# Maxima for a softmax: TensorE transposes replaced by VectorE's 32x32 block transposes, with four partial values a query

## The chip, the core and the metric

The kernel runs on one core of one Trainium2 chip. A core has five engines that run beside each other, each with its own in-order stream of instructions: TensorE (PE; its weight loads are listed as PEld), VectorE (DVE), ScalarE (ACT), GpSimd (POOL) and SyncE (SP). In this kernel SP issues all DMAs. An engine waits for another through semaphores, and whatever stands behind a waiting instruction on the same engine waits too. The metric is device time in microseconds (us); lower is better.

## What is computed

Cross-attention, then a state-space mixer, then a routed low-rank layer, each added to `x` (8 sequences of 64 tokens, width 512). The change touches only the softmax of the cross-attention:

```python
    q = rmsnorm(hidden @ q_proj_w.T)            # 32 heads of 128
    k, v = context @ k_proj_w.T, context @ v_proj_w.T   # 8 key heads, 1601 keys
    scores = einsum('bhqd,bhkd->bhqk', q, rmsnorm(k)) / sqrt(128) + mask
    attn = softmax(scores)                      # over the 1601 keys
    out = einsum('bhqk,bhkd->bhqd', attn, v)
```

Softmax takes the maximum over the keys off every score before the exponential. All data is float32.

## The kernel before

**Units.** The attention is cut into 32 units, 4 pairs of key heads (`pr`) for each of 8 sequences (`b`), `pr` running fastest. A pass of the loop in `attend_all` does two things at once: it projects keys and values of unit n (nine "pieces", the P of the list below), and it does the attention of unit n-1. The order in which a pass is written is a list:

```python
    order = (
        "S00 P S01 P S02 P A0 D P S10 B0 P S11 P S12 V00 N A1 P V01 B1 F P P V10 V11".split()
    )
```

The digit after a letter is the half (0 or 1): one of the unit's two key heads, with 4 query heads x 64 queries = 256 query columns. S makes scores, A the maxima, B the softmax, V the product with the values. N and F are sums and factors for the norm of the keys, and D is the division by the softmax's sums.

**The framework's planner.** The list is not yet the order on the engines. Semaphores and buffers come from a tile framework. It takes the place in the program as a priority and puts each engine's instructions in order ahead of time, from its own estimate of when each is ready. On the chip that order is fixed: an engine does not pass over an instruction whose input is late.

**Scores (S, lines 526 to 542).** Keys lie on partitions, queries along the free axis: TensorE makes tiles of 128 keys x 256 queries (13 tiles for 1601 keys; PSUM buffer `psc`, two of them). VectorE multiplies each by the key's norm factor and adds the mask (L531) into `attn`, and keeps a running maximum of two tiles at a time (L540, L542).

**Maxima (A, lines 547 to 564).** L549 and L550 leave `mx`, 128 partitions x 256 queries: what is still to be taken is the maximum over the 128 partitions. TensorE transposes `mx` in two blocks of 128x128 into PSUM (`mtp`, L553), VectorE takes the maximum along the free axis and negates it (L555, `nm`), and a VectorE transpose (L558, 32x32 blocks) turns the column into four rows per block. SP writes the 256 values to a buffer in DRAM (L562, `max_d`) and, once the write has landed, loads them from there into all 128 partitions (L564, `nbs`, 128 KB).

**Softmax (B, lines 570 to 588).** ScalarE copies `nbs` to PSUM (L571, `nb`), VectorE adds it to four tiles at a time (L574, the last at L584), ScalarE takes the exponential (L578, L585), GpSimd sums over the tiles (L580 to L588).

**Buffers.** `mtp`, `nb` and the keys' squared sums `psn` (L414, copied out by ScalarE at L419) share one PSUM buffer, tag `tr` of the pool `ps3`, with a single copy.

**The projections around it.** A piece makes products in four PSUM banks (`pk_a` to `pk_d` for keys, L385; `pv_a` to `pv_d` for values, L445), and between them VectorE takes sums off (L359 `u`, L361 `t`, L377). The second half of a piece adds onto banks that these sums must have read: `pk_b` waits for L361, `pk_c` for L377. At the change from one sequence to the next, a pass also loads the next context (L826, `cx`, two loads of 768 KB, issued after A0 in the list, the other parts later in the pass) and VectorE forms sums of it (L849). These passes are called context passes here, and the others ordinary passes.

Of the kernel before, what the change touches and what calls it, by code (L numbers as in the profile page):

```python
# [9 lines left out]
F32 = mybir.dt.float32  # L10
AF = mybir.ActivationFunctionType
ALU = mybir.AluOpType
AX = mybir.AxisListType
PSUM = bass.MemoryType.PSUM

P = 128
# [37 lines left out]
def key_rows(t):  # L54

    return P if t < 2 * NHT else KV - 2 * NHT * P
# [57 lines left out]
def load_ln_exp(nc):  # L114

    return nc.scalar.preload_act_table_set("natural_log_exp_and_others")
# [186 lines left out]
def attend_all(  # L303
# [7 lines left out]
    nc = tc.nc  # L311

    wk2 = ctx.enter_context(tc.tile_pool(name="xa_wk2", bufs=2))
    small = ctx.enter_context(tc.tile_pool(name="xa_small", bufs=4))
    kp = ctx.enter_context(tc.tile_pool(name="xa_k", bufs=2))
    vp = [ctx.enter_context(tc.tile_pool(name="xa_v0", bufs=1))]
    ap_ = ctx.enter_context(tc.tile_pool(name="xa_attn", bufs=2))
# [3 lines left out]
    ps3 = ctx.enter_context(tc.tile_pool(name="xa_ps3", bufs=1, space=PSUM))  # L321
# [3 lines left out]
        pass  # L325


    negated = [wk2.tile([P, 2, 32], F32, tag=f"nm{hh}", name=f"nm{hh}", bufs=1) for hh in range(2)]
    for nm in negated:
        nc.gpsimd.memset(nm, 0.0)  # L330

# [1 line left out]
    marks = {}  # L333
# [172 lines left out]
    def attention(u):  # L506
# [37 lines left out]
        def maxima(hh):  # L544

            s = st[hh]
            at, lr = s.at, key_rows(NKT - 1)
            mx = ap_.tile([P, 256], F32, tag="mx", name="mx")
            nc.vector.tensor_tensor(mx, s.mx2[:, 0, :], s.mx2[:, 1, :], ALU.max)  # L549
            nc.vector.tensor_tensor(mx[:lr], mx[:lr], at[:lr, NKT - 1, :], ALU.max)  # L550
            tp = ps3.tile([P, 2, P], F32, tag="tr", name="mtp")
            for i in range(2):
                nc.tensor.transpose(tp[:, i, :], mx[:, i * P : (i + 1) * P], c.ident)  # L553
            nm = negated[hh]
            nc.vector.tensor_reduce(nm[:, :, 0], tp, axis=AX.X, op=ALU.max, negate=True)  # L555

            turned = small.tile([P, 2, 32], F32, tag="nmt", name="nmt")
            nc.vector.transpose(  # L558
                turned.rearrange("p i q -> p (i q)"), nm.rearrange("p i q -> p (i q)")
            )  # L560
            row = u.rows.maxima[hh]
            nc.sync.dma_start(out=row.rearrange("(i a q) -> a i q", i=2, q=32), in_=turned[0:P:32])  # L562
            s.nbs = ap_.tile([P, 256], F32, tag="nbs", name="nbs")
            marks["load"] = nc.sync.dma_start(out=s.nbs, in_=row.rearrange("(o q) -> o q", o=1).broadcast_to([P, 256]))  # L564

        def softmax(hh):
            s = st[hh]
            at, lr = s.at, key_rows(NKT - 1)

            nb = ps3.tile([P, 256], F32, tag="tr", name="nb")  # L570
            nc.scalar.copy(nb, s.nbs)  # L571
            sm2 = ap_.tile([P, 2, 256], F32, tag="sm2", name="sm2", bufs=1)
            for k in range(0, NKT - 1, 4):
                nc.vector.tensor_tensor(  # L574
                    at[:, k : k + 4, :], at[:, k : k + 4, :],
                    nb.unsqueeze(1).to_broadcast([P, 4, 256]), ALU.add,
                )
                nc.scalar.activation(at[:, k : k + 4, :], at[:, k : k + 4, :], AF.Exp)  # L578
                if k == 0:
                    nc.gpsimd.tensor_tensor(sm2, at[:, 0:2, :], at[:, 2:4, :], ALU.add)  # L580
                else:
                    for i in (k, k + 2):
                        nc.gpsimd.tensor_tensor(sm2, sm2, at[:, i : i + 2, :], ALU.add)  # L583
            nc.vector.tensor_tensor(at[:lr, NKT - 1, :], at[:lr, NKT - 1, :], nb[:lr], ALU.add)  # L584
            marks["exp"] = nc.scalar.activation(at[:lr, NKT - 1, :], at[:lr, NKT - 1, :], AF.Exp)  # L585
            s.sm = ap_.tile([P, 256], F32, tag="sm", name="sm")
            nc.gpsimd.tensor_tensor(s.sm, sm2[:, 0, :], sm2[:, 1, :], ALU.add)
            nc.gpsimd.tensor_tensor(s.sm[:lr], s.sm[:lr], at[:lr, NKT - 1, :], ALU.add)  # L588
# [43 lines left out]
        def divide():  # L632
# [9 lines left out]
            S00=lambda: score(0, s0), S01=lambda: score(0, s1), S02=lambda: score(0, s2),  # L642
            S10=lambda: score(1, s0), S11=lambda: score(1, s1), S12=lambda: score(1, s2),
            A0=lambda: maxima(0), A1=lambda: maxima(1),
            B0=lambda: softmax(0), B1=lambda: softmax(1),
            V00=lambda: outputs(0, 0), V01=lambda: outputs(0, 1),
            V10=lambda: outputs(1, 0), V11=lambda: (outputs(1, 1), sums()),
# [8 lines left out]
    for n in range(NPR * B):  # L656
        u = Unit()
# [108 lines left out]
    for n in range(len(units) + 1):  # L766
        if n < len(units):
            u = units[n]
            pieces, keys_norms, keys_factors = projections(u)
            todo = ahead(n + 1)  # L770
        else:
            u, pieces = None, last_pieces
# [127 lines left out]
@with_exitstack  # L900
def cross_attention(ctx, tc, c, x, ctxT, lastT, maskT, wq, wk, wv, wo):

    nc = tc.nc
    load_ln_exp(nc)
    big = ctx.enter_context(tc.tile_pool(name="xa_big", bufs=1))
    dram = ctx.enter_context(tc.tile_pool(name="xa_dram", bufs=1, space=bass.MemoryType.DRAM))
    qw = big.tile([P, 1], F32, name="qw")

    nc.vector.tensor_scalar(
        qw, c.qnw, c.knw, 1.0 / math.sqrt(HD), op0=ALU.mult, op1=ALU.mult  # L910
    )
    mask_sb = big.tile([P, NKT, S], F32, name="mask_sb")

    last_keys = big.tile([P, DC, B], F32, name="last_keys")
    q_d = [dram.tile([B, P, PQ, S], F32, name=f"q_d_{pr}") for pr in range(NPR)]
    rs_d = [dram.tile([4, NT], F32, name=f"rs_d_{n}") for n in range(HQ // 4)]
    s_d = {
        (name, pr): dram.tile([P, 4, 2, HD], F32, name=f"{name}_s_d_{pr}")
        for name in ("wk", "wv") for pr in range(NPR)
    }  # L920
    o_d = [dram.tile([P, PQ, B, S], F32, name=f"o_d_{pr}") for pr in range(NPR)]
    v1_d = [dram.tile([B, 2 * HD], F32, name=f"v1_d_{pr}") for pr in range(NPR)]

    rows_d = []
    for i in range(3):
        r = Consts()
        r.keys = dram.tile([4, NHT * P], F32, name=f"keys_d_{i}")
        r.last = dram.tile([4, LAST], F32, name=f"last_d_{i}")
        r.maxima = [dram.tile([256], F32, name=f"max_d_{i}_{hh}") for hh in range(2)]
        r.sums = dram.tile([2, 256], F32, name=f"sums_d_{i}")  # L930
        rows_d.append(r)

    with tc.tile_pool(name="xa_ctx", bufs=1) as ctxp, tc.tile_pool(name="xa_w", bufs=1) as wpool:
        loads = Loads(nc, ctxp, wpool, ctxT, wk, wv, s_d)
        queries_loaded = project_queries(tc, c, x, wq, qw, q_d, rs_d)
        full = NKT - 1

        def load_mask():
            nc.sync.dma_start(
                out=mask_sb[:, :full, :], in_=maskT[: full * P, :].rearrange("(t p) q -> p t q", p=P)  # L940
            )
            nc.sync.dma_start(out=mask_sb[: KV - full * P, full, :], in_=maskT[full * P :, :])
            nc.sync.dma_start(out=last_keys, in_=lastT.rearrange("(dc p) b -> p dc b", p=P))

        return attend_all(
            tc, c, x, loads, mask_sb, load_mask, last_keys, q_d, o_d, v1_d, rows_d, wo, queries_loaded
        )
# [403 lines left out]
@with_exitstack  # L1351
def perceiver(
    ctx: ExitStack, tc, x_in, ctxT, lastT, maskT, wq, wk, wv, wo, small, w_in, w_out, w_ra, b_w, out,
):
    nc = tc.nc
    cpool = ctx.enter_context(tc.tile_pool(name="consts", bufs=1))
    x = cpool.tile([P, NTT, D], F32, name="x")
    for tt in range(NTT):
        nc.sync.dma_start(out=x[:, tt, :], in_=x_in[tt * P : (tt + 1) * P, :])
    c = make_consts(nc, cpool, small)  # L1360
    done = cross_attention(tc, c, x, ctxT, lastT, maskT, wq, wk, wv, wo)
    mixer_and_routed(tc, c, x, done, w_in, w_out, w_ra, b_w, out)
# [52 lines left out]
```

## Time and profile before

| | |
|---|---|
| median of 3 runs | 2828.47 us (2826.2 to 2830.78) |
| the profiled execution | 2826.02 us, of which the traced span is 2824.3 us |
| VectorE busy | 1745.4 us, 62% of the span |
| ScalarE busy | 726.6 us, 26% |
| GpSimd busy | 833.9 us, 30% |
| chain that ended last, by engine | PE 83%, DVE 6%, DMA 2%, ACT 1% |
| same, lines of the attention | `pav` L596 12%, `psc` L526 11%, `nbs<-max_d` 2%, L574 1% |
| running maxima, L542, 128x512 | 818 ns mean, 256 of them |
| L549, 128x256 | 437 ns mean, 64 of them |
| `nb` copy on ScalarE, L571 | 376 ns mean, 64 of them |
| bytes moved by DMA | 206.02 MB, 73 GB/s over the span |

Busy time is the sum of instruction durations on an engine. Matmuls are pipelined: their listed duration is from start to end of one, longer than the distance between two starts in a row. The chain of waits goes back from the last instruction to whatever released it; its shares say where time is on the path that sets the end. A row of the groups gives a source line, the engine, the output and inputs, shapes and count, then total and mean time, then the engine's idle time ahead of it and what ended it. Times in a timeline are us from the start of the span.

### The profile page before, as it was taken

The page shows a single profiled execution, that of the slowest core. Times are in us where ns is not written, and L with a number is a line of the kernel's source. Part 1 is how long each engine was busy: PE and PEld are TensorE (multiplying, and loading weights), DVE is VectorE, ACT ScalarE, POOL GpSimd, SP SyncE. Part 2 cuts the span into 40 slices and gives each one's busy share as a digit, 9 for nine tenths or more (in the row PEclk, how much of TensorE's full clock was granted, in tenths as well). Part 3 has the DMA queues.
Part 4 walks back from the last instruction along what each step waited for, and adds up shares of the span by engine and source line. Part 5 has one row for each costly group of instructions (what it writes and reads, how often), then busy time and mean ns, then how long its engine had stood idle before and what let it go on. Part 6 is the DMA issues. An engine that isn't in the chain of part 4 may idle for free.

```text
span 2824.3 us, 38454 instructions
## 1 busy us (share of the span) xinstructions
PE 2788.6 (99%) x14972; PEld 1980.9 (70%) x14972; DVE 1745.4 (62%) x3059; ACT 726.6 (26%) x1314; POOL 833.9 (30%) x786
## 2 busy tenths in 40 slices
PE   9899999999999999999999999999999999999998
PEld 7677777777777777777777777777777554444444
DVE  4556676676667666665666676667665416444555
ACT  3322223222222222232222222222222103222222
POOL 4323223222222332223222222322232223433431
PEclk9999999999999999999999999999999999999999
DMA  4822232232113122312311131122212441112200
GB/s 164 276 78 57 76 74 53 53 94 53 46 46 97 46 54 79 74 48 58 94 50 50 46 95 47 46 83 76 48 46 72 146 160 38 53 53 78 79 16 15
DMA packets 277230, 206.02 MB, mean 73 GB/s; under 512 B 155676, under 2 KB 240538, under 8 KB 276026
## 3 DMA queue, kind: packets, MB, share of 16 engines
q1 hardware_dynamic: 277050, 203.57, 25.2%
q8 instruction: 119, 1.95, 0.3%
q14 instruction: 61, 0.50, 0.1%
HBM read 180.87 MB, written 22.66 MB: 72 GB/s over the span
## 4 chain that ended last, share of the span: by engine, by line
PE 83%; DVE 6%; DMA 2%; ACT 1%; issue 0%; POOL 0%; SPq 0%; ACTq 0%; DVEq 0%
PE pav L596 12%; PE psc L526 11%; PE pj L1105 8%; PE pv_a L445 6%; PE pv_b L445 6%; PE pv_c L445 5%; PE pk_a L385 5%; PE pk_b L385 5%; PE pk_c L385 5%; PE mo L1213 4%; PE pv_d L445 3%; PE pk_d L385 2%; PE psn L414 2%; DMA nbs<-max_d 2%; DVE attn L574 1%; PE pvl L468 1%
## 5 line engine op out<-in xcount | busy, mean ns | idle before, releaser
L531 DVE SCALAR_TENSOR_TENSOR attn<-psc,rk,mask_sb 128x256 f32<-128x256 f32 (+1 forms) x832 | 363.4, 473 | 190.5 <-PE psc L526 188.1
L580 POOL TENSOR_TENSOR sm<-attn 128x512 f32<-128x512 f32 x64 | 82.0, 1281 | 1147.6 <-ACT attn L578 1147.6
L596 PE MATMUL pav<-attn,v 128*128 128x256 f32 (+1 forms) x1664 | 384.3, 381 | 0.0
L526 PE MATMUL psc<-q,kT 128*128 128x256 f32 x1536 | 371.5, 381 | 0.0
L596 PEld LDWEIGHTS pav<-attn,v 128*128 128x128 f32 (+1 forms) x1664 | 311.1, 190 | 55.4 <-issue 9.6
L583 POOL TENSOR_TENSOR sm<-sm,attn 128x512 f32<-128x512 f32 x256 | 339.8, 1328 | 29.4 <-DVE attn L574 10.6
L526 PEld LDWEIGHTS psc<-q,kT 128*128 128x128 f32 x1536 | 286.3, 190 | 82.4 <-issue 36.0
L1105 PE MATMUL pj<-mx_xnT,w_in 128*128 128x512 f32 x640 | 296.3, 603 | 1.3 <-DVE acc L1122 1.3
L574 DVE TENSOR_TENSOR attn<-attn,nb 128x1024 f32<-128x1024 f32 x192 | 224.7, 1216 | 68.2 <-ACT nb L571 67.9
L445 PEld LDWEIGHTS pv_a<-wv,cx 128*128 128x128 f32 x1536 | 195.5, 191 | 48.2 <-issue 41.4
L578 ACT ACTIVATE attn<-attn 128x1024 f32<-128x1024 f32 x192 | 202.5, 1058 | 71.3 <-DVE attn L574 68.5
L445 PE MATMUL pv_a<-wv,cx 128*128 128x128 f32 x1536 | 212.7, 279 | 0.0
L542 DVE TENSOR_TENSOR mx<-mx,attn 128x512 f32<-128x512 f32 x256 | 209.5, 818 | 2.0
L1105 PEld LDWEIGHTS pj<-mx_xnT,w_in 128*128 128x128 f32 x640 | 115.2, 190 | 129.4 <-issue 124.7
L385 PE MATMUL pk_a<-cx,wk 128*128 128x417 f32 (+1 forms) x512 | 193.3, 500 | 0.8 <-ACT qrs L110 0.8
L396 ACT ACTIVATE ksq<-kT 128x834 f32<-128x834 f32 (+1 forms) x128 | 109.0, 871 | 159.1 <-DVE kT L377 159.1
L637 POOL TENSOR_TENSOR o<-o,f 128x512 f32<-128x512 f32 x31 | 39.4, 1272 | 306.7 <-DMA f<-sums_d 206.3
L385 PEld LDWEIGHTS pk_a<-cx,wk 128*128 128x128 f32 x512 | 97.2, 190 | 46.1 <-issue 20.8
L1217 DVE SCALAR_TENSOR_TENSOR x<-mo,rs,x 128x512 f32<-128x512 f32 x32 | 24.0, 751 | 165.1 <-PE mo L1213 110.4
L1213 PE MATMUL mo<-w_out,y 128*128 128x512 f32 x256 | 118.1, 597 | 0.0
L571 ACT COPY nb<-nbs 128x256 f32<-128x256 f32 x64 | 24.1, 376 | 324.4 <-DMA nbs<-max_d 324.4
L1122 DVE SCALAR_TENSOR_TENSOR acc<-pj,small_consts,acc 128x504 f32<-128x504 f32 (+1 forms) x144 | 103.9, 725 | 0.7
(220 smaller groups left out, 4230.8 us busy)
## 6 DMA issues: line engine op xcount, KB each, us to landing
wk<-in_wk SPq DMA_DIRECT2D x32, 512.0 KB
wv<-in_wv SPq DMA_DIRECT2D x32, 512.0 KB
w_in<-in_w_in SPq DMA_DIRECT2D x16, 1024.0 KB
wvs<-wv_s_d SPq DMA_DIRECT2D x28, 512.0 KB
wks<-wk_s_d SPq DMA_DIRECT2D x28, 512.0 KB
cx<-in_ctxT SPq DMA_DIRECT2D x16, 834.0 KB
cx<-in_ctxT SPq DMA_DIRECT2D x16, 768.0 KB
wq<-in_wq SPq DMA_DIRECT2D x16, 512.0 KB
```

Source lines behind the costliest of these rows:

```text
L385: nc.tensor.matmul(ps[:, :w], lhsT=u.wk[l][:, dc, :], rhs=u.cx.r[ch][r][:, dc, :], start=start and dc == 0, stop=dc == 1, skip_group_check ...
L396: nc.scalar.activation(sq[ch][:, :, half, :w], u.kT[:, :, half, lo:hi], AF.Square)
L445: nc.tensor.matmul(ps[:, i * HD : (i + 1) * HD], lhsT=u.cx.r[ch][r][:, dc, i * P : (i + 1) * P], rhs=u.wv[l][:, dc, :], start=start and i ...
L526: nc.tensor.matmul(ps[:rows, t - t2, :], lhsT=lhsT, rhs=qh, start=True, stop=True)
L531: nc.vector.scalar_tensor_tensor(out=s.at[:rows, t, :].rearrange("p (h q) -> p h q", h=GQ), in0=ps[:rows, t - t2, :].rearrange("p (h q) -> ...
L542: nc.vector.tensor_tensor(s.mx2, s.mx2, s.at[:, t2 : t2 + 2, :], ALU.max)
L574: nc.vector.tensor_tensor(at[:, k : k + 4, :], at[:, k : k + 4, :], nb.unsqueeze(1).to_broadcast([P, 4, 256]), ALU.add,)
L578: nc.scalar.activation(at[:, k : k + 4, :], at[:, k : k + 4, :], AF.Exp)
L583: nc.gpsimd.tensor_tensor(sm2, sm2, at[:, i : i + 2, :], ALU.add)
L596: nc.tensor.matmul(s.av[:, 0, :], lhsT=u.v[:rows, t, hh, :], rhs=s.at[:rows, t, :], start=t == 0, stop=t == NKT - 1,)
L1105: nc.tensor.matmul(pj, lhsT=G.w[:, dc, n, :], rhs=xnT[:, dc, :], start=dc == 0, stop=dc == DC - 1)
L1213: nc.tensor.matmul(po, lhsT=G.y[:, n, tt * P : (tt + 1) * P], rhs=G.wo[:, n, :], start=n == 0, stop=n == GC - 1,)
```

## The change

In A, the TensorE transposes (64 times two) are gone. VectorE transposes `mx` (128x256) in blocks of 32x32 in one instruction into a new SBUF tile `mxt`, and the reduction takes the maximum of each block's 32 columns. Since a block transpose stays within its group of 32 partitions, partition 32i+r, column j then holds the negated maximum of query 32j+r over the keys of partition group i alone: four partial values a query. A second block transpose (128x32 instead of 128x64) lays them out in rows, and SP writes all 128 rows of 32 values (16 KB instead of 1 KB, 128 pieces of 128 bytes instead of 8). The load brings, for each partition, four pieces of 1 KB (512 KB in all instead of 128 KB).

In B, ScalarE's copy is gone. VectorE takes the minimum of the four (they are negated) in two instructions: 128x512 within `nbs`, then 128x256 into the PSUM tile `nb`. `nbs` has one buffer of 4 KB per partition instead of two of 1 KB.

```diff
-    negated = [wk2.tile([P, 2, 32], F32, tag=f"nm{hh}", name=f"nm{hh}", bufs=1) for hh in range(2)]
+    negated = [wk2.tile([P, 32], F32, tag=f"nm{hh}", name=f"nm{hh}", bufs=1) for hh in range(2)]
...
-            tp = ps3.tile([P, 2, P], F32, tag="tr", name="mtp")
-            for i in range(2):
-                nc.tensor.transpose(tp[:, i, :], mx[:, i * P : (i + 1) * P], c.ident)
+
+            tp = ap_.tile([P, 256], F32, tag="mxt", name="mxt", bufs=1)
+            nc.vector.transpose(tp, mx)
             nm = negated[hh]
-            nc.vector.tensor_reduce(nm[:, :, 0], tp, axis=AX.X, op=ALU.max, negate=True)
-
-            turned = small.tile([P, 2, 32], F32, tag="nmt", name="nmt")
-            nc.vector.transpose(
-                turned.rearrange("p i q -> p (i q)"), nm.rearrange("p i q -> p (i q)")
-            )
-            row = u.rows.maxima[hh]
-            nc.sync.dma_start(out=row.rearrange("(i a q) -> a i q", i=2, q=32), in_=turned[0:P:32])
-            s.nbs = ap_.tile([P, 256], F32, tag="nbs", name="nbs")
-            marks["load"] = nc.sync.dma_start(out=s.nbs, in_=row.rearrange("(o q) -> o q", o=1).broadcast_to([P, 256]))
+            nc.vector.tensor_reduce(
+                nm[:, : 256 // 32], tp.rearrange("p (j k) -> p j k", k=32), axis=AX.X, op=ALU.max,
+                negate=True,
+            )
+
+            turned = small.tile([P, 32], F32, tag="nmt", name="nmt")
+            nc.vector.transpose(turned, nm)
+            rows = u.rows.maxima[hh]
+            nc.sync.dma_start(out=rows, in_=turned)
+            s.nbs = ap_.tile([P, 4, 256], F32, tag="nbs", name="nbs", bufs=1)
+            marks["load"] = nc.sync.dma_start(
+                out=s.nbs.rearrange("p i (o q) -> p i o q", o=1),
+                in_=rows.rearrange("(i o j) r -> o i (j r)", i=4, o=1)[:, :, :256]
+                .unsqueeze(2).broadcast_to([P, 4, 1, 256]),
+            )
...
             nb = ps3.tile([P, 256], F32, tag="tr", name="nb")
-            nc.scalar.copy(nb, s.nbs)
+            nc.vector.tensor_tensor(s.nbs[:, 0:2], s.nbs[:, 0:2], s.nbs[:, 2:4], ALU.min)
+            nc.vector.tensor_tensor(nb, s.nbs[:, 0], s.nbs[:, 1], ALU.min)
...
-        r.maxima = [dram.tile([256], F32, name=f"max_d_{i}_{hh}") for hh in range(2)]
+        r.maxima = [dram.tile([P, 32], F32, name=f"max_d_{i}_{hh}") for hh in range(2)]
```

## The prediction

> **What bounds the kernel now.** First the page's busy times, then the rows of the lines that the change touches, out of the groups kept apart by shape:
>
> ```profile
> PE 2788.6 (99%) x14972; PEld 1980.9 (70%) x14972; DVE 1745.4 (62%) x3059; ACT 726.6 (26%) x1314; POOL 833.9 (30%) x786
> ...
> L553 PE MATMUL mtp<-ident,mx 128*128 128x128 f32 x128 | 24.4, 273 | 0.0
> ...
> L555 DVE TENSOR_REDUCE nm<-mtp 128x2 f32<-128x256 f32 x64 | 27.2, 425 | 81.5 <-PE mtp L553 81.5
> ...
> L571 ACT COPY nb<-nbs 128x256 f32<-128x256 f32 x64 | 24.1, 376 | 324.4 <-DMA nbs<-max_d 324.4
> ```
>
> TensorE is the bound over the span, and the transposes are its work. The waits in the other two rows (DVE for the transposes, ACT for the load) count only where TensorE in turn waits for them. Where it does, the chain of waits shows:
>
> ```profile
> 994.92 2.16 PE pav L596 x10
> ...
> 1059.38 2.16 PE pav L596 x10
> ...
> 1107.16 5.52 DMA nbs<-max_d
> 1113.19 3.48 DVE attn L574 x3
> 1122.06 1.95 DVE cs L849
> ...
> 1190.08 2.16 PE pav L596 x10
> ```
>
> From one `pav` mark to the same mark a pass later it is 1059.38 - 994.92 = 64.46 us with nothing but PE between: an ordinary pass, and the trace has 21 that agree to 0.01. The next mark comes at 1190.08, 130.70 us on: 64.47 and a context pass of 66.23, in which the chain leaves PE for the load and then for DVE. Eight context passes lie 1.4 to 3.0 us over 64.47. So the change is worth its PE time in ordinary passes and its load-and-DVE time in context passes.
>
> Third, the timelines, once for an ordinary A0 and B0 and once for a context pass:
>
> ```profile
> 1166.22 0.42 DVE L550 TENSOR_TENSOR mx<-mx,attn 65x256 f32<-65x256 f32 x1
> ...
> 1170.49 0.38 PE L553 MATMUL mtp<-ident,mx 128*128 128x128 f32 x2
> ...
> 1170.71 0.83 PE L445 MATMUL pv_a<-wv,cx 128*128 128x128 f32 x6
> ...
> 1171.64 0.55 SPq L562 DMA_DIRECT2D max_d<-nmt  x1
> ...
> 1173.25 0.32 SPq L564 DMA_DIRECT2D nbs<-max_d  x1
> ...
> 1176.24 0.38 ACT L571 COPY nb<-nbs 128x256 f32<-128x256 f32 x1 [4.18 <-DMA nbs<-max_d]
> ...
> 1176.79 1.21 DVE L574 TENSOR_TENSOR attn<-attn,nb 128x1024 f32<-128x1024 f32 x1
> ...
> 1181.79 0.59 DVE L361 TENSOR_TENSOR t<-u,pk_b 128x417 f32<-128x417 f32 x1
> ...
> 1184.53 1.56 PE L385 MATMUL pk_b<-cx,wks 128*128 128x417 f32 x4
> ```
>
> ```profile
> 1107.16 0.46 SPq L564 DMA_DIRECT2D nbs<-max_d  x1
> ...
> 1113.19 3.48 DVE L574 TENSOR_TENSOR attn<-attn,nb 128x1024 f32<-128x1024 f32 x3 [1.83 <-ACT nb L571]
> ...
> 1125.43 0.62 PE L526 MATMUL psc<-q,kl 128*66 128x256 f32 x2 [1.32 <-DVE attn L531]
> ```
>
> **What goes from TensorE.** The pair of transposes starts at 1170.49, the next matmul at 1170.71: 0.22 us a pair, 64 x 0.22 = 14.1 us. A rule is to be weighed here. The Trainium skill, "TensorE: Matmul & The Clock Gate", Part 4: PE-mode transpose, puts a transpose at about 275 ns in a kernel. The row has 273, but these overlap: by the rule 128 x 0.275 = 35 us would go, by the distance of the starts 14.1. I take 14.1.
>
> **The chain of A.** Now L550 ends at 1166.64 and the write is issued at 1171.64, 5.00 us later (A1 of an ordinary pass: 2.29), because `mtp` waits until ScalarE has emptied `psn` from the shared buffer (that copy runs 1169.86 to 1170.34). The new chain waits for no one: transpose 128x256, reduction, transpose 128x32. The 128x64 transpose takes 245 ns. If a column costs what it costs DVE elsewhere (L542's median 681 ns for 512 columns against L549's 426 for 256: 1.0 ns), 128x256 is 0.44 and 128x32 is 0.21. With 0.43 for the reduction: 1.08, with gaps 1.15. Two evacuations of the value piece (0.55 each) may come between at A0. So the write goes out 1.15 (A1) to 2.2 us (A0) after L550: 1.1 and 2.8 earlier than now.
>
> **The write and the load.** Neither shape is in the trace. Now, write to load is 1.61 us and load to `nb` 2.99 (3.3 at A1). The packet records bound the write: 8 pieces of 128 B are over 1.26 us after issue, a store of 128 pieces of 2 KB 1.66, one of 1024 pieces of 256 B 2.54. So +0 to +1.3; with 128 pieces it is nearest to the second, +0.35. The load of 512 pieces of 1 KB has a twin, `wv`: 3.08 us to its last packet where `nbs` takes 2.87. But `wv` reads different rows at 52 ns a piece and `nbs` the same row at 83 on median; 24 more pieces for each of 16 queues at 83 would be +2.0. So +0.2 to +2.0; I take +0.4, since the `nbs` pieces follow each other at issue speed in both cases. Landing in the ordinary B0: 1166.64 + 2.2 + 1.95 + 3.35 = 1174.15, ahead of the 1176.24 of now.
>
> **The minima on DVE.** 128x512 at 0.68 (L542's median; mean 0.82 with GpSimd beside it), 128x256 at 0.43: 1.1 to 1.25 us for the 0.38 copy on ACT. With +0.40 in A (1.08 for 0.67) DVE gets 1.5 us a half, 64 x 1.5 = 96 us. A rule speaks against exactly this: "VectorE: DVE Perf Modes", Rules for kernel authors, sends 128x128 transposes to TensorE and asks for few DVE operations. Were DVE the bound, the sum would be 96 - 14 = 82 us slower. By this trace DVE is 62% busy and TensorE 99%, so PE time counts in full, and DVE time where DVE runs without a gap.
>
> That is the case at B0. In the ordinary pass DVE is busy from 1175.2 to 1188.4 but for about 0.2 us. Behind the waiting minimum on its in-order stream stand the evacuations of the value piece, the four score tiles of S10, then L574, L359, L361. Until the end of L584 now: 1181.11 (start of L359). After: DVE free at 1173.5, load at 1174.15, about 8 us of work with the minima, of which the 0.55 of an evacuation runs while it waits: 1181.6 to 1182.2, so 0.5 to 1.1 us late. L361 then ends by 1183.5; `pk_b` needs it at 1184.53 - 0.22 = 1184.3: covered. The tightest place is `psc<-q,kl` at 1189.49, whose buffer is free at about 1189.3 now; `pav` matmuls that are ready can be put ahead of it. I charge 0.2 us of new stall: 0.44 - 0.2 = 0.24 gained, times 24 (21 ordinary passes, 3 at the ends) = 5.8.
>
> B1: 1.1 earlier, then +0.35, +0.4 and +0.75 for minima against copy: 0.4 late. V10 starts at 1206.84 and needs the first exponential of 1202.8 and the last of 1205.65 nine matmul pairs into it: slack near 2.8. Hidden. ScalarE loses only a copy it waited for.
>
> Context passes: now `cx` (768 KB) is issued at 1106.68, just ahead of the load at 1107.16, which takes 5.62. With the write 2.8 earlier, the load is due at about 1100.41 + 2.2 + 1.95 = 1104.6, before `cx` can go (its buffer is read by TensorE until about 1106), and lands at about 1108. The minima go into gaps that DVE has there; L574 starts near 1111.9 instead of 1113.19: 1.25 earlier, of the 1.3 to 1.8 that PE waits in such a pass. With A1's pair, about 1.2 net: 8 x 1.2 = 9.6.
>
> Sum: 5.8 + 9.6 = **15.4 us faster**. From the profiled 2826.0 that is 2810.6; the median of the runs is 2.4 above the profiled one, so 2813.
>
> **Rivals.**
> 1. *Gain eaten.* The stall at the score tiles is 0.6 instead of 0.2 (DVE has no spare gap there), and the context passes recover only half: 24 x -0.16 + 8 x 0.6 = 1, so 2827. For: DVE is dense. Against: `pav` matmuls can fill.
> 2. *The wait heads DVE's line* (slower). ACT waited 324.4 us for this load at no cost; now DVE does. If the planner believes in an early load, it puts the minimum before S10's tiles, and a late landing holds all behind it. From about 1175.6 on (1.45 later than I take) the stall exceeds the 0.44: 1175.6 + 7.45 - 1181.11 = 1.94 late, less 1.5 of cover. At 1176.3, within both bounds of the DMAs, it is 1.14 of stall, net 0.7 x 24 = 17, and some 3 in context passes: 2848. For: in the last pass DVE stood 7.7 us before L574 with score tiles ready behind it. Against: in ordinary passes the planner put L574 behind the tiles, near its true time.
> 3. *`cx` stays ahead of the load.* Then the landing at 1112.7 moves out by 0.4 to 2 and the minima come on top: about +2 x 8 = 16 against 5.8 gained: 2839.
>
> **Numbers.** Main case 0.48, rivals 0.17, 0.25, 0.10. No change means within 0.2% (5.7 us), what runs of this spread can tell: faster 0.5, same 0.16, slower 0.34. Range 2804 (no stall in ordinary passes, 10.5 + 11 us, with spread) to 2848; the main case alone 2804 to 2821.
>
> **What would show it.** No `mtp`; ordinary marks 64.03 to 64.3 apart; write within 2.2 us of L550; load to first minimum 3.3 to 3.8; load issued before `cx`. Wrong if: ordinary marks over 64.5 apart with PE idle before `psc` or `pk_b` behind DVE, a DVE wait for the load with score tiles ready, or a load of 5 us.

## The result, and the profile after

The changed kernel takes 2907.4 us (median of 4 runs, 2901.1 to 2908.2) against 2829.1: a ratio of 1.0273, 95% interval 1.0255 to 1.0291. It is slower by 2.7%, where I forecast 0.5% faster; the profiled execution has a span of 2905.4 us, 81.1 over the one before.

The busy times first, then the rows of the changed lines, as in the prediction (in the changed kernel L553 is the turn of `mx`, L576 and L577 are the minima, L580 the subtraction that was L574):

```profile
PE 2816.4 (97%) x14844; PEld 1975.9 (68%) x14844; DVE 1828.4 (63%) x3251; ACT 705.3 (24%) x1250; POOL 855.3 (29%) x786
...
L576 DVE TENSOR_TENSOR nbs<-nbs 128x512 f32<-128x512 f32 x64 | 44.3, 692 | 179.2 <-DMA nbs<-max_d 179.2
...
L553 DVE STREAM_TRANSPOSE mxt<-mx 128x256 f32<-128x256 f32 x64 | 28.0, 438 | 0.9
L577 DVE TENSOR_TENSOR nb<-nbs 128x256 f32<-128x256 f32 x64 | 27.4, 427 | 1.1
...
L561 DVE STREAM_TRANSPOSE nmt<-nm 128x32 f32<-128x32 f32 x64 | 13.3, 207 | 0.9
```

The operations cost what the sum had for them: 438, 207, 692 and 427 ns. TensorE has 128 matmuls less and is busier in sum by 28 us: its matmuls are stretched by waits and, below, by a slower clock. The new entry is at the end of the L576 row: VectorE, not ScalarE, now stands idle for the load, 179.2 us in all.

What TensorE itself waited for in the attention, from 200 us to 2330 us; before, then after:

```profile
PE psc L526 <- DVE attn L531: 10.5, 8, 1.4
PE pk_b L385 <- DVE t L361: 2.3, 3, 1.0
```

```profile
PE pav L626 <- POOL sm L594: 24.1, 13, 3.3
PE pk_b L385 <- DVE t L361: 16.4, 19, 2.0
PE psc L526 <- DVE attn L531: 12.6, 7, 2.0
PE pav L602 <- ACT attn L584: 5.6, 8, 1.0
PE pvl L481 <- DVE v L475: 5.0, 2, 2.5
```

The columns are the sum in us, how often, and the longest. Three lines are new or have grown, and they hang on one thing: the softmax is late. Its sums on GpSimd (L594), its exponentials on ScalarE (L584), and what stands behind the minimum on VectorE (L361) come late with it. The wait for L531 is little longer than before, and that for L475 is there with a small load too (2.6 and 3.9 us in two runs below).

The timeline shows how. An ordinary B0, in which L550 ended at 1211.42:

```profile
1213.30 0.32 SPq L563 DMA_DIRECT2D max_d<-nmt  x1
...
1215.14 0.53 SPq L420 DMA_DIRECT2D keys_d<-kss  x1
1215.77 0.39 SPq L565 DMA_DIRECT2D nbs<-max_d  x1
...
1218.62 1.89 PE L526 MATMUL psc<-q,kT 128*128 128x256 f32 x8
...
1220.99 0.69 DVE L576 TENSOR_TENSOR nbs<-nbs 128x512 f32<-128x512 f32 x1 [1.61 <-DMA nbs<-max_d]
1221.60 1.66 DVE L531 SCALAR_TENSOR_TENSOR attn<-psc,rk,mask_sb 128x256 f32<-128x256 f32 x4
...
1223.17 0.42 DVE L577 TENSOR_TENSOR nb<-nbs 128x256 f32<-128x256 f32 x1
...
1228.72 0.58 DVE L361 TENSOR_TENSOR t<-u,pk_b 128x417 f32<-128x417 f32 x1
```

The write is out early, 1.9 us after L550, as forecast. The load is issued at 1215.77 and its first reader starts at 1220.99: 5.2 us, where the sum had 3.35. (The issue, too, is some 0.9 us later than the write allows: SP has `keys_d` ahead of it, which waits for ScalarE's copy.) And the order is that of rival 2: L576 stands ahead of S10's four score tiles. TensorE begins those scores at 1218.62; VectorE, idle for the load, gets to them at 1221.60.

Where the 81 us lie, the marks tell: here the first of the two sums' matmuls that end a pass (L626). By them the eight context passes lose 29 us together, the eight stretches behind them 35, the other fifteen passes 15.5 (about 1.0 each), and the start of the span 1.8. But a mark stands ahead of the second of these matmuls, and it is this one that waits for GpSimd:

```profile
1190.17 0.62 PE L626 MATMUL pav<-sm,ones 128*32 128x256 f32 x2
1193.84 0.62 PE L626 MATMUL pav<-sm,ones 128*32 128x256 f32 x2 [3.05 <-POOL sm L594]
```

Eight such waits, 22 us in all, come directly behind the mark that ends a context pass. Counted with them, the context passes lose 51 of the 81 us and what is behind them 13.

### The profile page after: what moved, and what is told of

It reads as the page before. It is cut to its first block, busy times and chain, and to the rows that moved or that the text cites. A ratio compares the mean times of both kernels' runs of the same rounds, so it can differ in the third digit from the quotient of the medians.

```text
span 2905.4 us, 38127 instructions
## 1 busy us (share of the span) xinstructions
PE 2816.4 (97%) x14844; PEld 1975.9 (68%) x14844; DVE 1828.4 (63%) x3251; ACT 705.3 (24%) x1250; POOL 855.3 (29%) x786
## 5 line engine op out<-in xcount | busy, mean ns | idle before, releaser
L531 DVE SCALAR_TENSOR_TENSOR attn<-psc,rk,mask_sb 128x256 f32<-128x256 f32 (+1 forms) x832 | 359.7, 471 | 130.6 <-PE psc L526 126.1
L602 PE MATMUL pav<-attn,v 128*128 128x256 f32 (+1 forms) x1664 | 391.6, 386 | 5.7 <-ACT attn L584 5.6
L589 POOL TENSOR_TENSOR sm<-sm,attn 128x512 f32<-128x512 f32 x256 | 354.9, 1386 | 20.8 <-ACT vl L474 0.2
L584 ACT ACTIVATE attn<-attn 128x1024 f32<-128x1024 f32 x192 | 200.4, 1056 | 253.8 <-DVE attn L580 250.9
L580 DVE TENSOR_TENSOR attn<-attn,nb 128x1024 f32<-128x1024 f32 x192 | 222.6, 1213 | 1.1
L445 PE MATMUL pv_a<-wv,cx 128*128 128x128 f32 x1536 | 203.7, 279 | 0.0
L576 DVE TENSOR_TENSOR nbs<-nbs 128x512 f32<-128x512 f32 x64 | 44.3, 692 | 179.2 <-DMA nbs<-max_d 179.2
L385 PE MATMUL pk_b<-cx,wks 128*128 128x384 f32 (+1 forms) x256 | 100.3, 514 | 16.7 <-DVE t L361 16.4
L357 ACT COPY p<-pk_a 128x384 f32<-128x384 f32 x64 | 31.6, 494 | 316.3 <-PE pk_a L385 315.2
```

What stands on the lines that cost most here:

```text
L385: nc.tensor.matmul(ps[:, :w], lhsT=u.wk[l][:, dc, :], rhs=u.cx.r[ch][r][:, dc, :], start=start and dc == 0, stop=dc == 1, skip_group_check ...
L445: nc.tensor.matmul(ps[:, i * HD : (i + 1) * HD], lhsT=u.cx.r[ch][r][:, dc, i * P : (i + 1) * P], rhs=u.wv[l][:, dc, :], start=start and i ...
L531: nc.vector.scalar_tensor_tensor(out=s.at[:rows, t, :].rearrange("p (h q) -> p h q", h=GQ), in0=ps[:rows, t - t2, :].rearrange("p (h q) -> ...
L580: nc.vector.tensor_tensor(at[:, k : k + 4, :], at[:, k : k + 4, :], nb.unsqueeze(1).to_broadcast([P, 4, 256]), ALU.add,)
L602: nc.tensor.matmul(s.av[:, 0, :], lhsT=u.v[:rows, t, hh, :], rhs=s.at[:rows, t, :], start=t == 0, stop=t == NKT - 1,)
```

## The experiments

Three theories. **Load**: the fourfold load takes 5 us and more, and that lateness costs the time. **Wait**: a wait moved from ScalarE to VectorE, with the minima, costs it however short it is. **Turn**: the chain of maxima on VectorE, and the order that the planner makes around it, costs it. The first four runs cross three choices: who transposes, how much is loaded, who waits.

**The turn alone.** One of the four partial rows is loaded, and ScalarE copies it.

```diff
-            s.nbs = ap_.tile([P, 4, 256], F32, tag="nbs", name="nbs", bufs=1)
+            s.nbs = ap_.tile([P, 256], F32, tag="nbs", name="nbs")
...
-                out=s.nbs.rearrange("p i (o q) -> p i o q", o=1),
-                in_=rows.rearrange("(i o j) r -> o i (j r)", i=4, o=1)[:, :, :256]
-                .unsqueeze(2).broadcast_to([P, 4, 1, 256]),
+                out=s.nbs, in_=rows[0:8].rearrange("(o j) r -> o (j r)", o=1).broadcast_to([P, 256])
...
-            nc.vector.tensor_tensor(s.nbs[:, 0:2], s.nbs[:, 0:2], s.nbs[:, 2:4], ALU.min)
-            nc.vector.tensor_tensor(nb, s.nbs[:, 0], s.nbs[:, 1], ALU.min)
+            nc.scalar.copy(nb, s.nbs)
```

> Of the change, only the turn: block transposes on VectorE, all 128 rows written, but one of the four partial rows (1 KB a partition, 128 KB in all) is loaded and ScalarE copies it to PSUM as before. The maximum is then taken over the keys of one partition group of 32 alone, so the shift under the exponential differs. Load theory (the fourfold load, 5.0 to 5.6 us from issue to the first minimum where I took 3.35 to 3.8, costs the time): about 2812 us, the 15 us gained that I forecast, load 3 us. Wait theory (the wait and the minima on VectorE cost it): 2812 too. Turn theory (the longer chain of maxima on VectorE and the order planned around it cost it): 2860 or more.

Measured: 2811.95 us, ratio 0.9937 (0.9921 to 0.9954). So the turn theory falls: without the large load the turn brings 17 us, close to what I forecast for the whole. The load takes 3.0 us (A0) and 3.4 (A1) to its reader; ordinary passes are 64.03 us apart. The small `nbs` also has its two buffers back, but that is not the cause: from write to load it is 2.45 us at A0 and 1.53 at A1 with one buffer as with two, so no load waited for a buffer.

**The fourfold load, ScalarE waiting.**

```diff
-            nc.vector.tensor_tensor(s.nbs[:, 0:2], s.nbs[:, 0:2], s.nbs[:, 2:4], ALU.min)
-            nc.vector.tensor_tensor(nb, s.nbs[:, 0], s.nbs[:, 1], ALU.min)
+            nc.scalar.copy(nb, s.nbs[:, 0])
```

> As the changed kernel, fourfold load included, but without the two minima: ScalarE copies the first of the four loaded rows to PSUM. Same shift as in the run with the turn only. Load theory: most of the loss stays, 2870 to 2890, with VectorE idle before the subtraction instead of before the minimum. Wait theory: about 2820, since ScalarE waits and VectorE passes on.

Measured: 2853.66 us, 1.0086 (1.0071 to 1.0102). The load alone costs 42 us against the run above, less than the load theory's 2870, far more than the wait theory allows. What VectorE waits for, in its list of waits, shows why handing the wait to ScalarE helps only in part:

```profile
DVE attn L579 <- ACT nb L576: 191.9, 64, 8.4
```

VectorE does not wait for the load itself any more, but for ScalarE's `nb` behind it: in every one of the 64 halves, 192 us in all (84 us in the turn alone).

**The minima and the wait on VectorE, small load.** Against the turn alone:

```diff
-            nc.scalar.copy(nb, s.nbs)
+            two = ap_.tile([P, 2, 256], F32, tag="two", name="two", bufs=1)
+            each = s.nbs.unsqueeze(1).to_broadcast([P, 2, 256])
+            nc.vector.tensor_tensor(two, each, each, ALU.min)
+            nc.vector.tensor_tensor(nb, two[:, 0], two[:, 1], ALU.min)
```

> As the changed kernel, but one partial row is loaded (128 KB) and VectorE makes two minima of the same sizes (128x512, 128x256) out of it, so it waits for the load itself. Load theory: 2820 to 2835 (minima of 1.1 us, load of 3 us). Wait theory: 2875 to 2900, since the small load is still waited for at the head of VectorE's line.

Measured: 2811.77 us, 0.9940 (0.9925 to 0.9955). The same as with ScalarE's copy. The 72 us of minima and the wait at the head of VectorE's line cost nothing when the load is there in 3.0 to 3.3 us. The wait theory falls as it stood. This run and the change differ in the load and in the order that the planner made for it: here both minima and the first subtraction stand ahead of S10's score tiles, in the change only the first minimum does. So the fourfold load, with the order planned around it, is what costs the 96 us between them.

**The same edit in the kernel before** (TensorE transposes, small load).

> The kernel before with its TensorE transposes and its load of 128 KB, and one edit: ScalarE's copy is replaced by the two minima of 128x512 and 128x256 on VectorE. The result is the reference's. Load theory: 1.1 us of VectorE time more a half, 2830 to 2845. Wait theory: 2880 or more.

Measured: 2834.99 us, 1.0021 (1.0014 to 1.0027): 6 us, within the load theory's range. Here A0's write is 5 us after L550, so there is less time to hide the minima in. It is no test of a wait at the head of the line: the planner put the minima behind S10's score tiles in 31 of 32 passes.

**Half the load.** Two of the four rows, minima of the same sizes.

```diff
-            s.nbs = ap_.tile([P, 4, 256], F32, tag="nbs", name="nbs", bufs=1)
+            s.nbs = ap_.tile([P, 2, 256], F32, tag="nbs", name="nbs", bufs=1)
...
-                in_=rows.rearrange("(i o j) r -> o i (j r)", i=4, o=1)[:, :, :256]
-                .unsqueeze(2).broadcast_to([P, 4, 1, 256]),
+                in_=rows.rearrange("(i o j) r -> o i (j r)", i=4, o=1)[:, :2, :256]
+                .unsqueeze(2).broadcast_to([P, 2, 1, 256]),
...
-            nc.vector.tensor_tensor(s.nbs[:, 0:2], s.nbs[:, 0:2], s.nbs[:, 2:4], ALU.min)
+            nc.vector.tensor_tensor(s.nbs, s.nbs, s.nbs, ALU.min)
```

> As the changed kernel, but two of the four partial rows are loaded (256 KB), with the two minima kept at their sizes (the first of the tile with itself); the shift covers two partition groups. Load theory: load of 3.6 to 4 us; between 2812 and 2907. If the loss grows evenly with the lateness, about 2840; if there is cover until the load passes some 4 us, about 2815.

Measured: 2822.21 us, 0.9978 (0.9968 to 0.9988), load to reader 3.3 and 3.6 us. Closer to cover than to even growth, and the first 0.3 us already cost 10.

**Own rows.** The same 512 pieces, but each partition reads different bytes. What the maxima do not fill of these rows is set to zero once, before the first pass.

```diff
-            nc.sync.dma_start(out=rows, in_=turned)
+            nc.sync.dma_start(out=rows[:, 0, :32], in_=turned)
...
-            marks["load"] = nc.sync.dma_start(
-                out=s.nbs.rearrange("p i (o q) -> p i o q", o=1),
-                in_=rows.rearrange("(i o j) r -> o i (j r)", i=4, o=1)[:, :, :256]
-                .unsqueeze(2).broadcast_to([P, 4, 1, 256]),
-            )
+            marks["load"] = nc.sync.dma_start(out=s.nbs, in_=rows[:, :, :256])
...
-        r.maxima = [dram.tile([P, 32], F32, name=f"max_d_{i}_{hh}") for hh in range(2)]
+        r.maxima = [dram.tile([P, 4, 264], F32, name=f"max_d_{i}_{hh}") for hh in range(2)]
```

> As the changed kernel, the same 512 pieces of 1 KB a load, but each partition reads rows of its own in DRAM (512 KB in all, zeros but for the 32 columns that the pass writes) instead of all reading the same 4 KB; so the shift is not the maximum. If pieces of the same rows are what makes the load slow: first to last packet 2.0 us instead of 4.0, as the weight loads of the same shape, load to minimum about 3.4, and 2815 to 2835. If it is the number of pieces: load 5 us and about 2900.

Measured: 2849.45 us, 1.0067 (1.0050 to 1.0084), between the two answers. By the packet records the load is 2.33 us from first to last piece instead of 4.00, so most of the slowness comes with the shared rows; its first piece comes 0.3 later, and load to reader is 4.1 and 4.4 us. So of the change's 96 us over the small load, some 58 come with the shared rows; the other 38 come with four times the pieces and bytes, which this run does not separate. Both figures hold a change of order, too: in context passes A1's write leaves 1.2 us after L550 with the small load, 2.7 here and mostly 4.3 in the change (medians). Most ordinary passes here are still 64.03 us apart: a load of 4.1 to 4.4 us is hidden in them, and the loss is in the context passes and their sums.

**Where the minima stand.** The planner's order in B0 is overruled: minima behind S10's scores and their first maximum.

```diff
-                    nc.vector.tensor_tensor(s.mx2, s.at[:, 0:2, :], s.at[:, 2:4, :], ALU.max)
+                    marks["scored"] = nc.vector.tensor_tensor(
+                        s.mx2, s.at[:, 0:2, :], s.at[:, 2:4, :], ALU.max
+                    )
...
+            with behind(marks["scored"] if hh == 0 else None):
+                nc.vector.tensor_tensor(s.nbs[:, 0:2], s.nbs[:, 0:2], s.nbs[:, 2:4], ALU.min)
+                nc.vector.tensor_tensor(nb, s.nbs[:, 0], s.nbs[:, 1], ALU.min)
```

> As the changed kernel, with one order written out: in B0 the two minima may stand on VectorE only behind the four score tiles of S10 and their first maximum. Nothing is left out. If the place at the head of VectorE's line is what makes the late load dear (54 us more than with ScalarE waiting): 2855 to 2875. If it is lateness alone, wherever the wait stands: 2895 to 2910.

Measured: 2865.83 us, 1.0134 (1.0119 to 1.0149): 41 us back. So the order made the late load nearly twice as dear: 96 us over the small load with it, 54 without. Not all of it is the place in B0. Between the two profiled executions 12 us are regained in the fifteen ordinary passes, where that place is what got better, and 25 in the context passes, where the new plan also let A1's write go earlier (2.9 us after L550 for 4.3, medians). TensorE's waits for `pk_b` are gone; what is left is in the sums and exponentials:

```profile
PE pav L629 <- POOL sm L597: 24.5, 11, 3.4
PE pav L605 <- ACT attn L587: 10.1, 8, 2.1
...
PE psc L526 <- DVE attn L531: 2.1, 6, 0.4
```

**The fourfold load in the kernel before.** The row of 1 KB is loaded four times.

```diff
-            s.nbs = ap_.tile([P, 256], F32, tag="nbs", name="nbs")
-            marks["load"] = nc.sync.dma_start(out=s.nbs, in_=row.rearrange("(o q) -> o q", o=1).broadcast_to([P, 256]))
+            s.nbs = ap_.tile([P, 4, 256], F32, tag="nbs", name="nbs", bufs=1)
+            marks["load"] = nc.sync.dma_start(
+                out=s.nbs,
+                in_=row.rearrange("(o i q) -> o i q", o=1, i=1).broadcast_to([P, 4, 256]),
+            )
...
-            nc.scalar.copy(nb, s.nbs)
+            nc.scalar.copy(nb, s.nbs[:, 0])
```

> The kernel before, TensorE transposes and small write included, with one edit: the same 1 KB row is loaded four times into each partition (512 pieces, 512 KB) and ScalarE copies the first. The result is the reference's. Load theory: the load is late here too, 5 to 5.5 us to the copy, and A0 writes 3 us later than in the changed kernel, so at least the 42 us that the fourfold load cost behind the block transposes: 2870 to 2890. If the load only hurts together with the changed order or the wait on VectorE: within 10 us of the kernel before.

Measured: 3079.71 us, 1.0881 (1.0863 to 1.0899), far beyond the load theory's 2890. The load was slower than I expected: 6.88 us from first to last piece, 8.2 and 8.5 us to the copy. All 512 pieces come from one row here, from four in the change. The mechanism is the one of the load theory (TensorE waits 78 us for L361, 44 for the exponentials, 36 for GpSimd's sums); the load's length in the expectation was wrong. The clock has a part in it: the records show 106 us at half clock, by my estimate 53 of the 251 us lost.

**Folding before the write.** If four rows in the load are the cost, the four values can be brought together before it. The reduced maxima are only 8 columns wide. Behind the write stand the load of 128 KB and ScalarE's copy, as in the turn alone.

```diff
+            for n in (64, 32):
+                other = small.tile([64, 8], F32, tag=f"fold{n}", name=f"fold{n}")
+                nc.vector.tensor_copy(other[:n], nm[n : 2 * n, :8])
+                nc.vector.tensor_tensor(nm[:n, :8], nm[:n, :8], other[:n], ALU.min)
-            turned = small.tile([P, 32], F32, tag="nmt", name="nmt")
-            nc.vector.transpose(turned, nm)
+            turned = small.tile([32, 32], F32, tag="nmt", name="nmt")
+            nc.vector.transpose(turned, nm[:32])
...
-            nc.sync.dma_start(out=rows, in_=turned)
+            nc.sync.dma_start(out=rows[:8], in_=turned[:8])
```

> A version that computes the reference with the small load: the four partial values are brought together on VectorE before the write, by two copies of 8 columns to other partitions and two minima of 8 columns (64, then 32 partitions), then one 32x32 transpose, 8 rows written, 128 KB loaded, ScalarE copies. Load theory: as the run with the turn only, 2808 to 2820, faster than the kernel before. If a longer chain of maxima costs time: 2830 or more.

Measured: 2806.41 us, 0.9918 (0.9903 to 0.9932): faster than the kernel before by 22 us, and than the change by 101. It is a little below the expected 2808. The fold's four instructions take:

```profile
L562 DVE COPY fold<-nm 64x8 f32<-64x8 f32 x64 | 11.2, 175 | 2.1
L562 DVE COPY fold<-nm 32x8 f32<-32x8 f32 x64 | 10.2, 159 | 2.2
L563 DVE TENSOR_TENSOR nm<-nm,fold 64x8 f32<-64x8 f32 x64 | 10.2, 159 | 2.2
L563 DVE TENSOR_TENSOR nm<-nm,fold 32x8 f32<-32x8 f32 x64 | 9.8, 154 | 2.2
```

0.65 us a half, for minima of 1.12 and a load of a quarter the size. TensorE's waits in the attention, 13 us in the kernel before, are 3 in this one:

```profile
PE psc L526 <- DVE attn L531: 1.9, 5, 0.5
PE pav L628 <- POOL sm L596: 1.0, 2, 0.5
```

Set beside each other, the runs behind the block transposes with VectorE waiting and whatever order the planner made (load to first reader, mean of A0 and A1, and the median time):

| run | load, us | time, us |
|---|---|---|
| small load, minima | 3.1 | 2811.8 |
| two rows | 3.5 | 2822.2 |
| four rows, own to each partition | 4.3 | 2849.5 |
| the change: four shared rows | 5.5 | 2907.4 |

From one to the next it is 33, 34 and 48 us per us of load (from unrounded loads): with 64 halves, 52%, 53% and 75% of the delay is felt on the mean of all passes. The order changes along this line, so it is not the price of lateness alone. With ScalarE waiting, 3.2 to 5.4 us costs 2812 to 2854, 19 us per us.

## Why the prediction was wrong

**What failed** is one term of the sum: "So +0.2 to +2.0; I take +0.4, since the `nbs` pieces follow each other at issue speed in both cases." Measured, load to reader went from 3.2 and 3.3 to 5.4 and 5.5: +2.2, just past the upper bound. The pieces of `nbs` never followed each other at issue speed, and the trace before had it: by the packet records its 128 pieces take 1.89 us from first to last, the 512 of `wv` 2.00. A piece of the shared row came every 15 ns, one of `wv` every 4. At one row's pace 384 more pieces are +5.7 us; the fourfold load of one row measured +5.0, that of four rows +2.1. The 83 ns of my sum is what one piece takes; eight of them behind each other, the load of a queue in that sum, make 0.66 us and not 1.89, so the upper bound was not worked out from what sets the pace either, and that it came so near is luck.

With the load at 3 us the sum comes out: 2812 measured, twice, for 2813 predicted. Its terms are near too. By the marks of the run with small load and minima, context passes gain 11.5 us (9.6 in the sum) and the others 6.5 (5.8). The start and end of the span lose 4.8, which the sum did not have, so the last microseconds of the agreement are luck.

**The order** was the second thing, and it is that of rival 2: minimum ahead of the score tiles. The run with the order overruled gives it a share of 41 us, A1's order in context passes included. That the planner believed in an early load is rival 2's reading; the runs show the order and not the belief. My reason against it (in the kernel before the subtraction was planned behind the tiles) was weak, because the write now goes out 3 us earlier. Rival 2 gave 2848 because it counted the delay of `pk_b` in ordinary passes and only some 3 us in context passes. The waits of TensorE for GpSimd's sums and for the exponentials, 30 us of the list above, were missing, and 27 of them are those of context passes: I had called B1 "hidden" with 2.8 us of slack, on a delay of 0.4, from an ordinary pass. In context passes A1's last block transpose was also planned behind L359, which waits for TensorE, so that its write left 4.3 us after L550 in five of the eight; that I had not seen coming.

**What held.** The transposes cost TensorE 0.22 us a pair: ordinary passes went from 64.47 to 64.03, the 0.44 of the sum, wherever the load is small. The rule's 275 ns each (on its page a figure for bf16) would have made it 1.1 us a pass. The write left 1.6 to 1.9 us after L550 in ordinary passes, 1.15 to 2.2 forecast. 128 pieces of 128 bytes are cheap: 1.06 us to the last packet, and write to load 1.53 at A1 against 1.59. The minima are free if the load is in time, so VectorE's stretch at B0 had more room than the rule against more VectorE work suggests. The load does go out ahead of `cx` in context passes (1141.12 against 1142.84 in one of them), but there it took 6.9 us, `cx` beside it; the gain of 1.2 us a context pass became a loss of 3.6 by the marks, and of 6.4 with the sums' wait behind them.

## What to carry to other kernels

A load on the path from one engine to the next is priced by its slowest resource, and that can be the source: compare it with a twin that also reads shared rows, by pieces a us from first to last and not by what one piece takes, and if the trace has none, keep the pace of the shared row as the main case. When a copy moves to a busier engine its wait moves with it, and an ahead-of-time planner may put that wait anywhere: look at what is behind it in line. Four partial results are cheaper to combine while they are 8 columns wide than after they were broadcast.

## What the runs showed of the hardware

**Shared rows in a broadcast load.** Pieces of 1 KB, first to last packet, medians: 128 of one row 1.8 us, 256 of two rows 2.0, 512 of four rows 4.0, 512 of one row 6.9, 512 of own rows 2.3. That is 71, 126, 128, 74 and 220 pieces a us; `wv`, own rows again, has 256. One row gave the same pace whether 128 or 512 pieces were asked of it, and in the kernel before also with pieces of 2 KB (`f`, 128 of them in 1.9 us). Two and four rows gave the same pace as well, so the number of rows is not all of it. The loads also differ in where the rows lie (4 KB apart in the change, 1056 bytes with own rows) and in how much of them was just written; no run separates these, and why shared rows are slow stays open.

**The clock.** The mean granted clock was 0.993 in the change and 0.981 in the slowest run, 0.999 before. By the clock records it drops to half for stretches of 3.41 us, nine of them between 100 and 2400 us in the change (one of double length), 34 us in all; at half speed that is 17 us lost, by my estimate. The stretches around one of them, busy time of each engine in us (PE, PEld, DVE, ACT, POOL), then the clock, DMA share and GB/s:

```profile
1158.10:1161.52 3.42, 3.42 (x14) 2.28 (x12) 3.42 (x5) 0.00 (x0) 3.26 (x3) 1.00 0.56 170
1161.52:1164.93 3.41, 1.38 (x7) 1.12 (x7) 3.41 (x9) 1.70 (x2) 1.76 (x3) 1.00 0.43 137
1164.93:1168.34 3.41, 3.41 (x11) 1.91 (x14) 3.41 (x7) 0.00 (x0) 0.00 (x0) 0.50 0.26 77
1168.34:1171.75 3.41, 3.41 (x34) 2.92 (x27) 1.60 (x3) 0.99 (x2) 0.00 (x0) 1.00 0.01 4
```

In the second stretch TensorE is busy for 1.38 of 3.41 us, because of a wait for a score tile:

```profile
1163.66 0.62 PE L526 MATMUL psc<-q,kl 128*66 128x256 f32 x2 [2.03 <-DVE attn L531]
```

In the next the clock is 0.50. Two `pav` matmuls in a row start 427 ns apart inside such stretches and 216 outside (medians), so the matmuls do take twice as long. A wait of 2 us on TensorE can then cost another 1.7. The Trainium skill, "TensorE: Matmul & The Clock Gate", Part 1: The HAM clock gate, has windows of this length (about 3.4 us) and the halved clock after one that is idle; here a window that was 40% busy was enough, and the nine windows ahead of such stretches were 30 to 44% busy. Between 100 and 2400 us the kernel before, with no wait over 1.4 us in the attention, has no such stretch, and neither has the version that folds before the write.
